# Layer 0 of a four-layer vision network on one core: the norm's broadcast in two steps, and other due times for its streams and its last two samples

## Chip, core and metric

One core of a Trainium2 chip runs the whole program in one launch: all layers, batch 8, everything in fp32. The core has a matrix engine (TensorE, "PE" in the profile), a vector engine (VectorE, "DVE"), a scalar engine (ScalarE, "ACT"), a general engine (GpSimd, "POOL"), a queue engine that mostly issues transfers (SyncE, "SP"), and 16 DMA engines that move data between the memory and the on-chip buffers. The metric is device time in microseconds (us) of one launch; lower is better. Five runs give the time before.

## The reference, cut to what matters

The input is `x[8, 256, 32, 32]`; the output has the same shape. Layer 0, the only one that the change edits, is this (batch norms, `_bn`, are folded into scales and shifts):

```python
def _ln(x, w, b):
    r = lax.rsqrt(jnp.mean(x * x, axis=1, keepdims=True) + LN_EPS)
    return x * r * w[:, None, None] + b[:, None, None]

def _attention(x, ...):                     # 4 heads, key 32, value 64, N = 1024 positions
    qkv = _bn(_conv1x1(x, qkv_w), ...)
    attn = softmax(einsum('bhkn,bhkm->bhnm', q, k) * SCALE)
    out = einsum('bhdm,bhnm->bhdn', v, attn)
    pe = _bn(_dwconv3(v_img, pe_w), ...)    # 3x3, one filter per channel
    return _bn(_conv1x1(out + pe, proj_w), ...)

def _edffn(x, pi_w, dw_w, fft_p, po_w):
    x = _dwconv3(_conv1x1(x, pi_w), dw_w)   # 256 -> 1024 channels, then 3x3 per channel
    x = gelu(x[:, :512]) * x[:, 512:]
    x = _conv1x1(x, po_w)                   # 512 -> 256
    return irfft2(rfft2(patches8x8(x)) * fft_p)

def _forward(x, ...):
    x = x + gamma1 * _attention(_ln(x, norm1_w, norm1_b), ...)
    return x + gamma2 * _edffn(_ln(x, norm2_w, norm2_b), pi_w, dw_w, fft_p, po_w)
```

The norm `_ln` divides by the root mean square over the 256 channels: the sum runs over channels, and the result `r`, one number per position, is needed again in every channel. Layer 1 is a deformable convolution; further layers are attention and mixtures of experts. They matter here only because the first steps of layer 1 are issued while layer 0 ends.

## The kernel before

**Tiling.** A sample is a tile of 128 partitions by 2 x 1024: 256 channels in two halves (`KC = 2`), 1024 positions (`N`), worked on in halves of 512 (`HF`). Layer 0 is the function `fast0` (line 1110 on). It is written as Python generators: each is a *stream* of work for one sample, cut into *units* by `yield`. The streams are:

- `attention()` (`main`): for each sample, each half of the queries and each of 8 key tiles, two units: first the scores `s` (line 1393, four matmuls) and their exponentials `e` on ACT (L1399); then, one key tile late, the sums of the exponentials on DVE (`sum`, L1349 and L1353) and the values `A` (L1357, eight matmuls). That makes 32 units a sample (`T = 32`). After a half, `finish` runs beside the next steps: copy `A` to `av` (ACT), the denominators `D` (PE, L1372, from `sum`), their reciprocal `rr` by Ln and Exp (ACT, L1376 and the next), `av` times `rr` and `o` plus `av` (both DVE), two units later the projection `proj` (PE), the residual `x+av` (DVE, L1387) and the store to a DRAM buffer `mid`.
- `before_attention(b)`: load the sample (SP), norm it, project v, q and k (`qkv`, line 78 is the helper that issues it; the copies out are L1280), transpose v (`vT`, L1297), and do the 3x3 convolution of v on PE (`pe`, L1324) from a shifted copy `thrice` that twelve transfers on SP fill.
- `before_gates(b)`: load `mid`, norm it. `gates(b)`: eight blocks of 128 channels, each a 1x1 convolution (`pi`, PE), its copy out (`hp`, ACT, L1438) and a 3x3 depthwise convolution on DVE (`a`, first tap on ACT at L1239, eight taps on DVE at L1246). Pairs of blocks pass through gelu (ACT) into `st` and are multiplied by the partner block (DVE), then stored. In the last sample blocks 1 and 7 take the convolution on PE instead, as matmuls with diagonals (`dw`).
- `transforms(b)`: for each quarter of the sample, load the gated values `hc` and the residual `xc`, 1x1 convolution `po` (PE, L1491), forward transform `fwd` (PE), its gain (`u`, DVE, L1501), back transform `back` (PE, L1506), add to `xc` (DVE), store.

**The norm** is one helper for both places, `normed` (L1214 to L1235). It squares the sample (ACT, L1217); unit; sums the squares over channels with a matmul whose result lies as 64 equal rows per half (`ms`, PE, L1222) and takes `r` = 1/root by Ln and Exp (ACT, L93 and L94); unit; then for each half a matmul with a row of ones spreads a row of `r` to all partitions (`rb`, PE, L1231) and ACT copies it out (L1234) over the first square tile, which the profile names `v` in the first norm and `sq` in the second; last, one DVE product over the whole sample makes `xn` (L1235). All small results of PE in layer 0, `rb` and `D` and `back` and `pi` among them, take their bank of PSUM (PE's result memory) from one pool, `own["X"]`. It has two banks during attention, so a third result waits until one of the last two has been read out. After attention it has four.

**The order.** Nothing runs these streams in parallel by itself: the function `by_time` plays one unit after another, always of the stream whose *due time* is smallest, and adds the stream's *pace* to its due time. Time is counted in units of `main`, which starts at 0 with pace 1, so sample b's attention lies at 32b to 32b + 32, and the 256 units of all eight end near 258. The engines' instruction orders come from this order, through a scheduler that may still move an instruction ahead of others on its engine; only instructions marked `pinned` (gelu and its table load) keep their place. Each stream is given as (first due time, pace, generator):

```python
(T * (b - 1) - 2, 32 / 21, before_attention(b)) if b > 1 else (11 * b, 1.0, before_attention(b)),
(T * (b + 1) + 7.4, 0.9, before_gates(b)),
(T * (b + 1) + 10.5, 32 / 44, gates(b)),
(T * (b + 2) + 11.5, 2, transforms(b)),
```

So in the middle of the layer four samples are in work at once: while b attends, b+1 is being prepared, b-1 is in its norm and gates, and b-2 in its transforms. Ten units of `before_attention(0)` are played ahead of all (`next(streams[1][2])`). When `main` ends, attention's buffers are given back, and what is left of the last streams is played together with `net.head()`, due at T*B + 1 with pace 2. That is the first part of layer 1: its weight loads on SP and ACT's queue, memsets on POOL, the load of its first sample, that sample's first convolution (`c`) and group norm (`gn`), and so on, until a mark (`HOLD`) from which it needs layer 0's space.

Of the kernel before, what the change touches and what calls it, by code (L numbers as in the profile page):

```python
# [18 lines left out]
B = 8  # L19
# [117 lines left out]
def img(ap):  # L137
    return ap.rearrange("p (h w) -> p h w", w=IMG)
# [954 lines left out]
def by_time(streams, until=None):  # L1093


    due = [list(s) for s in streams]
    while due:
        d = min(due, key=lambda d: d[0])
        try:
            next(d[2])  # L1100
            d[0] += d[1]
        except StopIteration:
            due.remove(d)
            if d[2] is until:
                break
    return due
# [3 lines left out]
def fast0(net, io):  # L1110
# [7 lines left out]
    with ExitStack() as ctx, ExitStack() as att:  # L1118
# [35 lines left out]
        def bank(name):  # L1154
            return own["X"].tile([P, HF], F32, tag="X", name=name)
# [51 lines left out]
        def sc(i):  # L1207
            return s[:, i : i + 1]

        def sh(i):  # L1210
            return t[:, i : i + 1]

        def normed(xn, x, sq):

            squares = [sq(k) for k in range(KC)]
            for k in range(KC):
                nc.scalar.activation(squares[k], x[:, k, :], AF.Square)  # L1217
            yield
            ps = bank("ms")
            for k in range(KC):  # L1220
                for h in range(2):
                    nc.tensor.matmul(  # L1222
                        ps[64 * h : 64 * h + 64], lhsT=net.mean64, rhs=squares[k][:, bass.ts(h, HF)],
                        start=(k == 0), stop=(k == KC - 1),
                    )
            r = one.tile([P, HF], F32, tag="r", name="r")
            net.rsqrt(r, ps, net.eps6)
            yield
            for h in range(2):
                pr = bank("rb")  # L1230
                nc.tensor.matmul(  # L1231
                    pr, lhsT=net.unit[64 * h : 64 * h + 1, :], rhs=r[64 * h : 64 * h + 1, :], start=True, stop=True
                )
                nc.scalar.copy(squares[0][:, bass.ts(h, HF)], pr)  # L1234
            nc.vector.tensor_tensor(xn, x, squares[0].unsqueeze(1).to_broadcast([P, KC, N]), ALU.mult)  # L1235

        def depthwise(out, src, taps):
# [31 lines left out]
        def before_attention(b):  # L1269
            xn = aone.tile([P, KC, N], F32, tag="xn", name="xn")  # L1270
            nc.sync.dma_start(out=xn, in_=io.src[b])
            yield
            v = aone.tile([P, KC, N], F32, tag="v", name="v")
            yield from normed(xn, xn, lambda k: v[:, k, :])
            yield
            def projected(d, w, j, norm):
                for h in range(2):
                    ps = bank("qkv")
                    net.linear(ps, w, xn, bass.ts(j, P), bass.ts(h, HF))
                    nc.scalar.activation(d[:, bass.ts(h, HF)], ps, AF.Identity, scale=sc(norm), bias=sh(norm))  # L1280

            for c in range(KC):
                projected(v[:, c, :], wv, c, 2 + c)
                yield
            for d, (j, name) in ((qs, (0, "q")), (ks, (1, "k"))):
                d[b] = atwo.tile([P, N], F32, tag=name, name=name)
                projected(d[b], wqk, j, j)
                yield

            va = vas[b] = atwo.tile([P, NT, KC, P], F32, tag="va", name="va")  # L1290
            for t4 in range(0, NT, 4):
                for t2 in (t4, t4 + 2):
                    ps = bank("vT")
                    for i in range(2):
                        for c in range(KC):
                            lo = i * C + c * P
                            nc.tensor.transpose(ps[:, lo : lo + P], v[:, c, bass.ts(t2 + i, P)], net.ident)  # L1297
                    nc.scalar.copy(va[:, t2 : t2 + 2].rearrange("p t c d -> p (t c d)"), ps)
                yield

            o = os[b] = atwo.tile([P, KC, N], F32, tag="o", name="o")
            for c in range(KC):
                for h in range(2):

                    thrice = aone.tile([96, 4, HF], F32, tag="thrice", name="thrice")
                    edge = thrice[0:32, :, :IMG] if h == 0 else thrice[64:96, :, HF - IMG :]
                    nc.gpsimd.memset(edge, 0.0)  # L1307
                    for j in range(3):
                        n = HF * h + IMG * (j - 1)
                        lo, hi = max(0, n), min(N, n + HF)  # L1310
                        for g in range(4):
                            nc.sync.dma_start(
                                out=thrice[32 * j : 32 * j + 32, g, lo - n : hi - n],
                                in_=v[32 * g : 32 * g + 32, c, lo:hi],
                            )
                    yield
                    ps = bank("pe")
                    for j, s_ in enumerate((0, -1, 1)):
                        for g in range(4):
                            to, fr = (  # L1320
                                img(a)[:, :, max(0, -d_) : IMG - max(0, d_)]
                                for a, d_ in ((ps[32 * g : 32 * g + 32], s_), (thrice[:, g, :], -s_))
                            )
                            nc.tensor.matmul(  # L1324
                                to, lhsT=wpe[:96, c, s_ + 1, g, :], rhs=fr, start=(j == 0), stop=(j == 2)
                            )
                    nc.scalar.activation(
                        o[:, c, bass.ts(h, HF)], ps, AF.Identity, scale=sc(4 + c), bias=sh(4 + c)
                    )
                    yield  # L1330
                yield
# [87 lines left out]
        def before_gates(b):  # L1419
            xn = xs[b] = one.tile([P, KC, N], F32, tag="xn2", name="xn2")  # L1420
            nc.sync.dma_start(out=xn, in_=mids[b])
            yield

            def square(k):
                return five.tile([P, N], F32, tag="a", name="sq") if k else one.tile([P, N], F32, tag="sq", name="sq")

            yield from normed(xn, xn, square)
            yield
# [89 lines left out]
        T = 32  # L1518
        main = attention()
        streams = [(0, 1, main)]  # L1520
        for b in range(B):
            streams += [
                (T * (b - 1) - 2, 32 / 21, before_attention(b)) if b > 1 else (11 * b, 1.0, before_attention(b)),
                (T * (b + 1) + 7.4, 0.9, before_gates(b)),
                (T * (b + 1) + 10.5, 32 / 44, gates(b)),
                (T * (b + 2) + 11.5, 2, transforms(b)),
            ]
        for _ in range(10):
            next(streams[1][2])
        rest = by_time(streams, until=main)  # L1530
        att.close()
        own["X"], own["diag"] = io.pool(ctx, "f0t", 4, PSUM), io.pool(ctx, "f0d", 2)
        by_time(rest + [[T * B + 1, 2, net.head()]])

# [1422 lines left out]

GENERAL = [layer0, layer1, layer2_attention, layer2_ffn, layer3_attention, layer3_experts]  # L2960
LAYERS = [fast0, fast1, fast2, fast2f, fast3, fast3e]
LEAST, MOST = 1e-25, 1e25

# [265 lines left out]
```

## Time and profile before

| | us |
|---|---|
| five runs | 4276.41, 4264.66, 4272.24, 4272.69, 4262.2 |
| their median | 4272.24 |
| the profiled execution, its own time | 4274.56 |
| its span, first to last instruction | 4272.80 |
| layer 0 up to the last attention projection | 0 to 1279.39 |
| last projection to the last sample's first `pi` | 1279.39 to 1318.70 |
| one middle sample, `rb` to `rb` | 662.26 to 823.14 |

How to read the profile's lines, here and in the prediction: in the totals each engine has its busy time, its share of the span and its number of instructions; PEld is the loading of weights into PE, which lies beside its matmuls. In a timeline each line is start, duration, engine, source line, operation, "output<-inputs", partitions and elements, and how many like instructions the line stands for; a bracket gives the idle time of that engine just before, and what ended it. In a table of windows each line is a stretch of time, its length, then the busy time (and count) of PE, PEld, DVE, ACT and POOL, the mean granted clock of PE (1.00 is full speed), the busy share of the DMA engines, and the GB/s that they moved. The same view by whole stretches, for orientation:

```profile
340.00:501.00 161.00, 150.41 (x736) 57.65 (x732) 129.76 (x119) 88.47 (x112) 0.78 (x4) 0.96 0.26 82
501.00:662.00 161.00, 151.09 (x760) 58.67 (x753) 130.37 (x121) 93.42 (x119) 0.78 (x4) 0.98 0.27 85
662.00:823.00 161.00, 151.04 (x759) 58.55 (x753) 130.34 (x122) 93.36 (x119) 0.79 (x4) 0.98 0.27 85
823.00:984.00 161.00, 151.92 (x760) 58.67 (x755) 131.21 (x123) 94.84 (x120) 0.79 (x4) 0.98 0.27 85
```

The stretches are of one sample's length each. PE is busy for all but 8 to 11 us of 161, DVE for all but some 30.

### The profile page before, as it was taken

Reading aid. Unit: us, or ns where it says so; the run is one execution under the profiler, and the core shown is the slowest. Engines: PE = TensorE matmul, PEld = TensorE weight load, DVE = VectorE, ACT = ScalarE, POOL = GpSimd, SP = SyncE. Lnnn points to the kernel's source line nnn. Section 1 sums busy time; section 2 is a strip of 40 time slices with the busy share of each in tenths; the row PEclk is TensorE's granted clock in tenths of the full one; section 3 lists DMA queues with packets and bytes.
Section 4 is the critical chain, followed back from the end, with each engine's and each line's share of the span. In section 5 each row is a group of like instructions: output and inputs, shape, how many; then the busy total and the mean of one; then the engine's idle time right before and its main releaser. Section 6 shows DMA issues by size and latency. Waiting matters only on the chain. (4 is left out here: it accounts for less than half of the span.)

```text
span 4272.8 us, 53170 instructions
## 1 busy us (share of the span) xinstructions
PE 3968.6 (93%) x20006; PEld 1923.1 (45%) x20006; DVE 2295.6 (54%) x3979; ACT 2262.1 (53%) x3030; POOL 564.0 (13%) x645
## 2 busy tenths in 40 slices
PE   7999999999897899989999987989899999999997
PEld 3223333333333444445444444654344434445986
DVE  2368878878896577762222326853223333314455
ACT  3455555555554466653343345634656666666554
POOL 0000000000000000000000002531000151114763
PEclk9989999999998999999999998999999999999998
DMA  2222232232213101110010012541700041026676
GB/s 87 64 69 71 73 103 79 72 106 72 82 55 123 65 32 61 42 47 6 20 40 20 20 40 72 156 130 30 224 31 1 35 133 42 33 87 199 194 243 222
DMA packets 190637, 350.34 MB, mean 82 GB/s; under 512 B 24121, under 2 KB 134669, under 8 KB 178853
## 3 DMA queue, kind: packets, MB, share of 16 engines
q1 hardware_dynamic: 167124, 294.10, 21.2%
q0 software_dynamic: 19440, 46.45, 3.3%
q10 hardware_dynamic: 3808, 6.29, 0.4%
q8 instruction: 162, 2.65, 0.3%
q14 instruction: 103, 0.84, 0.1%
HBM read 175.15 MB, written 153.89 MB: 77 GB/s over the span
## 5 line engine op out<-in xcount | busy, mean ns | idle before, releaser
L2683 ACT ACTIVATE e<-s,five 128x1024 f32<-128x1024 f32 x512 | 539.3, 1111 | 281.2 <-PE s L2677 280.1
L1246 DVE SCALAR_TENSOR_TENSOR a<-hp,w_f_vec,a 128x961 f32<-128x961 f32 (+1 forms) x496 | 608.9, 1234 | 109.4 <-ACT a L1239 101.0
L2677 PE MATMUL s<-q,k 32*128 32x512 f32 x2048 | 348.9, 642 | 17.5 <-ACT e L2683 12.2
L1353 DVE TENSOR_TENSOR sum<-sum,e 128x1024 f32<-128x1024 f32 x192 | 230.8, 1221 | 154.4 <-ACT e L1399 154.4
L1399 ACT ACTIVATE e<-s 128x1024 f32<-128x1024 f32 x256 | 249.7, 1023 | 92.7 <-PE s L1393 83.1
L2661 PE MATMUL A<-e,v 128*32 128x512 f32 x2048 | 278.5, 608 | 0.0
L1357 PE MATMUL A<-e,va 128*32 128x512 f32 x2048 | 277.5, 624 | 0.0
L78 PE MATMUL pi<-xn,w_l_wpi 128*128 128x512 f32 x512 | 246.0, 622 | 14.8 <-ACT u L1500 9.2
L2677 PEld LDWEIGHTS s<-q,k 32*128 32x128 f32 x2048 | 111.5, 183 | 180.8 <-issue 96.5
L1393 PE MATMUL s<-q,k 32*128 32x512 f32 x1024 | 181.5, 645 | 2.4 <-ACT e L1399 2.4
L1724 PE MATMUL pos<-pos,w_f_sel 64*128 64x512 f32 x576 | 163.0, 631 | 8.5 <-ACT ay L1746 3.9
L78 PEld LDWEIGHTS pi<-xn,w_l_wpi 128*128 128x128 f32 x512 | 95.5, 197 | 154.1 <-issue 115.7
L1026 POOL DMA_INDIRECT res<-y,to x149 | 148.6, 998 | 106.9 <-DVE y L2854 49.4
L2830 PE MATMUL h<-xk,w 128*128 128x128 f32 x1192 | 149.0, 279 | 11.4 <-DVE xk L2816 11.4
L2830 PEld LDWEIGHTS h<-xk,w 128*128 128x128 f32 x1192 | 147.2, 195 | 16.3 <-DVE xk L2816 11.4
L2799 ACT COPY w<-w_l3f_w 128x512 f32 x149 | 92.6, 625 | 114.6 <-PE h L2830 110.6
L1438 ACT ACTIVATE hp<-pi,pib 128x512 f32<-128x512 f32 x128 | 87.2, 690 | 117.4 <-PE pi L78 117.4
L1324 PE MATMUL pe<-thrice,w_f_wpe 96*32 96x496 f32 (+1 forms) x768 | 129.9, 607 | 20.7 <-DMA thrice<-v 14.1
L1307 POOL MEMSET thrice<- 32x128 f32 x32 | 6.3, 196 | 1081.3 <-PE pe L1324 1061.3
L2850 PE MATMUL y<-w_l3f_w,hid 128*128 x596 | 144.3, 385 | 0.3 <-issue 0.3
L1357 PEld LDWEIGHTS A<-e,va 128*32 128x32 f32 x2048 | 61.8, 113 | 178.2 <-issue 177.3
L1026 POOL DMA_INDIRECT so<-xl,rows x128 | 129.6, 1013 | 93.6 <-issue 49.5
(408 smaller groups left out, 7067.7 us busy)
## 6 DMA issues: line engine op xcount, KB each, us to landing
x<-d SPq DMA_DIRECT2D x31, 1024.0 KB
xs<-so SPq DMA_DIRECT2D x73, 260.0 KB
so<-zero SPq DMA_DIRECT2D x5, 3380.0 KB
thrice<-v SPq DMA_DIRECT2D x256, 64.0 KB
gated<-st SPq DMA_DIRECT2D x32, 512.0 KB
hc<-gated SPq DMA_DIRECT2D x32, 512.0 KB
d<-x SPq DMA_DIRECT2D x16, 1024.0 KB
xl<-mox SPq DMA_DIRECT2D x64, 256.0 KB
```

Source lines behind the costliest of these rows:

```text
L78: self.nc.tensor.matmul(ps, lhsT=w[:, i, m], rhs=src[:, i, cols], start=(i == 0), stop=(i == k - 1))
L1026: made = self.nc.gpsimd.indirect_dma_start(**args)
L1246: nc.vector.scalar_tensor_tensor(to, fr, taps(t_), to, ALU.mult, ALU.add)
L1353: nc.vector.tensor_tensor(half, half, e[j], ALU.add)
L1357: nc.tensor.matmul(state["A"][32 * h : 32 * h + 32, c, :], lhsT=vas[b][:, kt, c, 32 * h : 32 * h + 32], rhs=e[h // 2][:, h % 2, :], start= ...
L1393: nc.tensor.matmul(ss[h // 2][:, h % 2], lhsT=ks[b][32 * h : 32 * h + 32, bass.ts(kt, P)], rhs=qs[b][32 * h : 32 * h + 32, bass.ts(gq, HF) ...
L1399: nc.scalar.activation(es[i][j], ss[j], AF.Exp, scale=SCALE)
L1724: nc.tensor.matmul(ps[:, bass.ts(h, HF)], lhsT=sel[r, t, xy, :], rhs=poss[b][r, :], start=True, stop=True)
L2661: nc.tensor.matmul(A[32 * h : 32 * h + 32], lhsT=v[:, kt, c * P + 32 * h : c * P + 32 * h + 32], rhs=e[:, h, :], start=first, stop=last,)
L2677: nc.tensor.matmul(ss[h // 2][:, h % 2], lhsT=k[32 * h : 32 * h + 32, c, bass.ts(kt, P)], rhs=q[32 * h : 32 * h + 32, c, bass.ts(hh, HF)], ...
L2683: nc.scalar.activation(e[:, 2 * j : 2 * j + 2], ss[j], AF.Square, scale=SCALE, bias=five)
L2830: nc.tensor.matmul(ps[:, j, m], lhsT=ws[j][:, k, bass.ts(m, P)], rhs=xk[:, j, k], start=(k == 0), stop=(k == KC - 1),)
```

## The change

It edits only `normed` and the end of `fast0`:

```diff
                 nc.scalar.copy(squares[0][:, bass.ts(h, HF)], pr)
+                if h == 0:
+                    yield
             nc.vector.tensor_tensor(xn, x, squares[0].unsqueeze(1).to_broadcast([P, KC, N]), ALU.mult)
...
             streams += [
-                (T * (b - 1) - 2, 32 / 21, before_attention(b)) if b > 1 else (11 * b, 1.0, before_attention(b)),
-                (T * (b + 1) + 7.4, 0.9, before_gates(b)),
+                (T * (b - 1) - 2, 32 / 22, before_attention(b)) if b > 1 else (11 * b, 1.0, before_attention(b)),
+                (T * (b + 1) + 7.4, 0.7, before_gates(b)),
                 (T * (b + 1) + 10.5, 32 / 44, gates(b)),
                 (T * (b + 2) + 11.5, 2, transforms(b)),
             ]
-        for _ in range(10):
+
+
+        for i, (at, pace) in enumerate(((T * (B - 1) + 10.5, 0.58), (T * B + 5.5, 2))):
+            streams[4 * (B - 2) + 3 + i] = (at, pace, streams[4 * (B - 2) + 3 + i][2])
+        for i, (at, pace) in enumerate(((T * B + 4.2, 0.7), (T * B + 7.3, 32 / 44), (T * B + 40.5, 2))):
+            streams[4 * (B - 1) + 2 + i] = (at, pace, streams[4 * (B - 1) + 2 + i][2])
+        for _ in range(11):
             next(streams[1][2])
         rest = by_time(streams, until=main)
         att.close()
         own["X"], own["diag"] = io.pool(ctx, "f0t", 4, PSUM), io.pool(ctx, "f0d", 2)
-        by_time(rest + [[T * B + 1, 2, net.head()]])
+        by_time(rest + [[T * B + 5, 2, net.head()]])
```

- In `normed` a unit ends behind the first half's broadcast and copy. Other streams' work may now stand between the two `rb` matmuls, and both norms have one unit more.
- `before_attention` gets the pace 32/22 for 32/21, its unit more in the same 32; `before_gates` gets 0.7 for 0.9. Eleven units are played ahead for ten.
- The streams of the last two samples are replaced. `gates(6)` starts when it did and goes at 0.58 for 0.727 a unit; `transforms(6)` starts 6 earlier. `before_gates(7)`, `gates(7)` and `transforms(7)` start 3.2, 3.2 and 3 earlier.
- The head of layer 1 is due at T*B + 5, behind the start of the last sample's norm at T*B + 4.2; before, it was due at T*B + 1, ahead of that norm's T*B + 7.4.

Line numbers of the kernel after are those of before plus 2 from line 1236 on, and plus 8 behind `fast0`.

## The prediction

> **What bounds the kernel now.** I read the page's totals first, then the layer's end by stages, then one sample of the middle engine by engine. The first two lines are the page's engine totals and its chain of waits: TensorE (PE) is busy nine tenths of the span and nothing else is near that.
>
> ```profile
> PE 3968.6 (93%) x20006; PEld 1923.1 (45%) x20006; DVE 2295.6 (54%) x3979; ACT 2262.1 (53%) x3030; POOL 564.0 (13%) x645
> ...
> PE 17%; DMA 2%; DVE 1%; issue 1%; POOL 0%; ACT 0%; DVEq 0%; SPq 0%; POOLq 0%; ACTq 0%
> ```
>
> So time can come only from places where PE waits or is given a slow clock. In layer 0 there are two kinds. The first recurs once per sample. The PE timeline (start, duration, operation, idle before and releaser), then VectorE's (DVE):
>
> ```profile
> 823.14 1.03 PE L1231 MATMUL rb<-r,unit 1*128 1x512 f32 x4
> 826.51 1.93 PE L1372 MATMUL D<-sum,unit 128*32 128x512 f32 x8 [2.33 <-ACT v L1234]
> 828.22 2.60 PE L1357 MATMUL A<-e,va 128*32 128x512 f32 x16
> 830.75 1.16 PE L1506 MATMUL back<-w_l_inv,u 128*128 128x128 f32 x8
> 831.84 1.14 PE L1393 MATMUL s<-q,k 32*128 32x512 f32 x8
> 832.91 3.70 PE L78 MATMUL qkv<-xn,w_f_wv 128*128 128x512 f32 x8
> ...
> 844.13 3.70 PE L78 MATMUL pi<-xn,w_l_wpi 128*128 128x512 f32 x8 [0.97 <-ACT v L1280]
> ```
> ```profile
> 822.93 0.69 DVE L1501 TENSOR_TENSOR u<-u,w_l_gam 128x512 f32<-128x512 f32 x1
> 824.19 5.05 DVE L1246 SCALAR_TENSOR_TENSOR a<-hp,w_f_vec,a 128x961 f32<-128x961 f32 x4 [0.57 <-ACT a L1239]
> 829.15 2.28 DVE L1235 TENSOR_TENSOR xn<-xn,v 128x2048 f32<-128x2048 f32 x1
> ```
>
> Both rb banks are full, so D waits 2.33 us for the copy out of the first. The product xn is ready at 831.4, and qkv never waits for it. After the gap PE is slow, as the granted clock (third column from the right) of two windows at the same place one sample earlier shows:
>
> ```profile
> 663.00:666.00 3.00, 0.67 (x6) 0.16 (x8) 2.62 (x3) 3.00 (x5) 0.00 (x0) 0.97 0.00 0
> 666.00:669.00 3.00, 3.00 (x20) 0.73 (x16) 2.96 (x3) 1.29 (x3) 0.00 (x0) 0.50 0.00 0
> ```
>
> D and A then take 4.24 us (826.51 to 830.75) against 2.72 elsewhere (588.96 to 591.68): 1.5 lost. The gap costs 3.85 us in all. The second kind is the end of the layer, by stages: last sample but one up to the last proj, the last norm, two stretches of the last sample's gates and transforms.
>
> ```profile
> 1183.94:1279.39 95.45, 85.80 (x416) 37.79 (x417) 89.75 (x85) 51.92 (x65) 0.00 (x0) 0.97 0.15 49
> 1279.39:1306.63 27.24, 10.85 (x26) 3.89 (x24) 23.25 (x28) 15.38 (x32) 6.01 (x6) 0.75 0.77 289
> 1306.63:1318.70 12.07, 10.74 (x34) 3.19 (x34) 3.43 (x7) 4.54 (x10) 0.00 (x0) 0.68 0.41 145
> 1318.70:1425.57 106.87, 98.39 (x301) 49.72 (x301) 70.52 (x75) 38.78 (x55) 0.00 (x0) 0.95 0.13 45
> 1425.57:1469.91 44.34, 39.80 (x186) 22.71 (x184) 12.38 (x28) 12.05 (x23) 0.50 (x2) 0.96 0.32 103
> ```
>
> DVE is busy 89.75 of 95.45 us in the first: it bounds that stage. In the second PE does 10.85 us of work in 27.24.
>
> **The change, part by part.** The built programs hold the same instructions; only their order differs, from the second norm on until layer 1's early matmuls (after that, by 1520 us, it is the same again). So the time moves by what PE's waits and slow clock change.
>
> *Two-step broadcast, first norm of samples 3 to 7.* The built orders (4 of 5 alike; sample 3 lacks back and xc):
>
> ```
> PE  before  rb rb D A*8 back s*4 qkv            after  rb D A*8 back rb s*4 A*8 qkv
> DVE before  u a*4 xn av xc o xc                 after  u a*3 sum av a o xc xc xn
> ```
>
> Removed: the 3.85 us. Added: on DVE xn now stands behind sum, av, o (1.13 each, 836.67 to 837.80) and two xc (0.34 each, 832.56 to 832.90): 4.1 later, from 833.2 to 835.4. All their inputs are there by then (rr and back's copy before 828.5), so it is queueing, and DVE cannot start earlier: it idles 0.57 at 824.19 for ScalarE (ACT). PE needs 823.14 + 2x0.53 + 0.88 + 1.83 + 1.09 + 1.07 + 1.85 = 830.9, then waits 4.4 for xn, then runs slow as above, 1.5. Net 4.4 + 1.5 - 3.85 = **+2.05** (bounds: +0.55 if the clock stays up; +2.6 if xn slips by half a product more).
>
> [...]
>
> *Behind it.* The second v projection moves to just behind pi (5 A between). It needs pi's bank, and ACT empties it only after the gelu block (838.50 to 843.30, 4.8), two e (1.8) and one hp (0.7), with 0.9 for v's copy: 8.2 after the first projection. PE has s, pi, 5 A: 5.8. Wait 2.4 for 0.97: **+1.4** (0 to +2.9 with a slow stretch).
>
> *Second norm (before_gates).* On DVE x+av (L1387) moves from behind 2 a to behind 6: 4.6 later. From its end to the squares, through two transfers on SP's queue, the trace has 692.71 to 700.76 = 8.05. So squares, ms and the queue behind ACT's squares (e, r, then rb's copy) come some 5 late, while PE, with k moved behind ms, arrives earlier; pi then waits for xn once more (about 2). Removed: 0.88 + 0.38 + 1.18 of waits with about 1.5 of slow clock. I take **+1.5** (0 to +5; nearest the low end, since PE's own lateness uses up part).
>
> *Pace 32/22.* po now stands in front of pe and covers the wait for thrice, 14.1 us over 9 places in the waits up to 1160 us; 0.5 to 1.8 in the middle samples: **-1.3**.
>
> Sum per sample 3.65 (from -1.3 to +9), five samples: **+18** (-6 to +45). Samples 0 to 2 have no gates beside the norm; their orders barely change: 0.
>
> *The plan of the last two samples.* With pace 0.58, nine more a and one more st pair stand on DVE before the last o: 98.4 us of DVE work from xn (1181.59) for 87.5 (the built orders, counted at the trace's steps: a 1.14, sum, av, o and x+av 1.13, st 0.61, u 0.60, xc 0.34, xn 2.21). With the 4.6 that DVE waits for its first a, o ends at 1284.6 for 1277.3. x+av follows 8 later as before, 1292.6. Then sample 6's own chain (1164.98 to 1183.94, 19) replaces the old 33.3 (1285.38 to 1318.70), because xn's load no longer follows five weight loads on SP. But it follows layer 1's x load and one d store that waits for xc (1.5), and three c matmuls stand between ms and rb whose weight load, now behind a gated store, took 8.9 from issue to c before: I add 4 in all (1.5 to 8). First pi of the last sample: 1315.6 for 1318.7, **-3** (-6 to +1). By then 9 off, one acc and two gn (9x0.27 + 1.06 + 0.3 = **+3.8**) are still to do. Up to pos before takes 151.2 (1318.70 to 1469.91) for 137.9 of matmul steps (start to start: pi 0.89, po 0.45, the diagonals' dw 0.87, fwd, z and acc 1.06, back and off 0.27, c 0.49, z_ 0.17); the new order needs no 12.95 us stop of DVE for back behind dw, and I give it 9 of loss for 13.3: **-4.3** (-9 to 0). Four z, eight z_ and four c (7.5) move behind pos, where PE idles 5.9 of 40: **-3**. Sum of the end **-6** (-18 to +6). POOL's order is unchanged; its memsets move with the head and nobody waits for them.
>
> Total +18 - 6 = +12. The profiled execution took 4274.56 (span 4272.80); with 12 it would be 4286.6. It lies 2.3 above the median of the five, so against that: **4284**.
>
> **Rivals.** *Even:* the moved waits cost what the old ones did; x+av and xn are late, but ACT and DVE catch up in DVE's 9 us of idle per sample. For it: the sums of +0.55 and 0 are within the bounds. Against: PE has no slack at the point itself. Then only the end counts: 4272 - 6 = 4266. *Faster:* the two old gaps go and xn's wait stays under 2, so each sample gains 2, and the hole of 27.24 us closes by another 6: 4272 - 10 - 12 = 4250. For it: that hole holds 16 us of idle. Against: DVE's order above. *Slower at the end too:* the last attention half is starved by DVE (D waits for sums behind nine more a, back for u), and the proj's 7 us never come back: -6 becomes +8, 4272 + 18 + 8 = 4298; it decides from the point where PE waits over 4 us for D.
>
> **Chances.** Forecast 0.45 (4280 to 4292), slower at the end 0.13, even 0.19, faster 0.23. A measurement of this kernel tells 0.2% (8.5 us) from no change. Slower 0.58, same 0.19, faster 0.23. The range reaches into both outer cases: 4250 to 4302.
>
> **What would show it.** Right: PE's wait at qkv for xn near 4 us in samples 4 to 7, none at D, a period (rb to rb, 662.26 to 823.14 before) of 163 to 165 us instead of 160.9, the last proj near 1285 plus the lag gathered, the 27.24 us hole shorter. Wrong: xn's wait under 2, a period at or below 160.9, or pi of the last sample over 10 us nearer to the last proj than I reckon.

## The result and the profile after

The changed kernel took 4289.18 us (median of 26 runs) where the kernel before, run beside it, took 4270.84 (median of 47): a ratio of 1.0040 with a 95% interval of 1.0033 to 1.0047, or +17 us (14 to 20). The forecast was +12 and slower. The direction and the size were right; the parts of the sum were not. The split broadcast cost less than half of what it was charged, and the new plan of the end, which was to give back 6, cost about 9 by the stages of the profile. The profiled execution of the changed kernel took 4285.93 us, its span 4284.1. So the two profiled executions differ by 11 us, where the medians differ by 18: that of before lies 3.7 us above its median, that of the changed kernel 3.3 below.

The page's engine totals and its chain of waits, after:

```profile
PE 3948.2 (92%) x20006; PEld 1930.0 (45%) x20006; DVE 2297.3 (54%) x3979; ACT 2263.5 (53%) x3030; POOL 563.2 (13%) x645
...
PE 3%; DMA 1%; DVE 1%; issue 0%; POOL 0%; DVEq 0%; ACT 0%; SPq 0%; POOLq 0%
```

The counts are those of before and the busy times hardly differ; PE is even busy 20 us less in a span 11 us longer. So the added time is waiting. The shares of the chain sum to 21% of the span before and to 5% after, and its pieces lie in the last fifth and the last twentieth; so it says nothing of layer 0.

The PE timeline of a middle sample at the first norm, then VectorE's (columns as before; the product xn, L1235 in the kernel before, is L1237 here):

```profile
819.47 1.90 PE L1359 MATMUL A<-e,va 128*32 128x512 f32 x16
821.30 1.16 PE L1508 MATMUL back<-w_l_inv,u 128*128 128x128 f32 x8
...
824.30 1.92 PE L1359 MATMUL A<-e,va 128*32 128x512 f32 x16
829.94 5.40 PE L78 MATMUL qkv<-xn,w_f_wv 128*128 128x512 f32 x8 [3.72 <-DVE xn L1237]
...
843.59 3.70 PE L78 MATMUL qkv<-xn,w_f_wv 128*128 128x512 f32 x8 [1.72 <-ACT hp L1440]
```
```profile
822.36 1.22 DVE L1351 TENSOR_TENSOR sum<-e 128x1024 f32<-128x1024 f32 x1
823.50 1.22 DVE L1381 TENSOR_TENSOR av<-av,rr 128x1024 f32<-128x1024 f32 x1
824.63 1.25 DVE L1248 SCALAR_TENSOR_TENSOR a<-hp,w_f_vec,a 128x992 f32<-128x992 f32 x1
825.79 1.22 DVE L1382 TENSOR_TENSOR o<-o,av 128x1024 f32<-128x1024 f32 x1
826.93 0.76 DVE L1515 TENSOR_TENSOR xc<-u,xc 128x256 f32<-128x256 f32 x2
827.60 2.29 DVE L1237 TENSOR_TENSOR xn<-xn,v 128x2048 f32<-128x2048 f32 x1
```

D no longer waits. In its place PE waits 3.72 us for xn, and the first projection then takes 5.40 us (granted clock 0.69 from 829.90 to 835.40) where the second takes 3.70 (1.00 from 843.50 to 847.30). The last copy of rb ends at 824.12 (ACT starts it at 823.54, 0.58 long), but DVE does av, a, o and xc before it turns to xn at 827.60: 3.5 us of queue.

All waits of PE over one sample, from the last proj of one to that of the next (line, releaser, total, times, longest), first before, then after:

```profile
PE D L1372 <- ACT v L1234: 2.3, 1, 2.3
PE pe L1324 <- DMA thrice<-v: 1.8, 1, 1.8
PE pi L78 <- ACT u L1500: 1.5, 1, 1.5
PE vT L1297 <- ACT sq L1234: 1.2, 1, 1.2
PE pi L78 <- ACT v L1280: 1.0, 1, 1.0
PE ms L1222 <- ACT k L1280: 0.9, 1, 0.9
```
```profile
PE qkv L78 <- DVE xn L1237: 3.7, 1, 3.7
PE ms L1222 <- ACT sq L1217: 2.3, 1, 2.3
PE qkv L78 <- ACT hp L1440: 1.7, 1, 1.7
PE pi L78 <- ACT u L1502: 1.5, 1, 1.5
PE pi L78 <- DVE xn L1237: 1.2, 1, 1.2
```

Of the old waits shown all but one went, and new ones came. With those too small to show, the waits of a sample went from 10.0 us to 10.9 here, and to 11.5 to 12.1 in the samples beside it.

The end by stages: last attention (last proj of sample 6 to last proj of sample 7), to the last sample's first pi, to layer 1's first pos, and to layer 1's last pos, where layer 1 ends. First before, then after:

```profile
1154.36:1279.39 125.03, 108.71 (x526) 44.29 (x527) 116.71 (x110) 65.09 (x81) 0.00 (x0) 0.94 0.20 69
1279.39:1318.70 39.31, 21.59 (x59) 7.08 (x57) 26.68 (x34) 19.92 (x41) 6.01 (x6) 0.73 0.66 245
1318.70:1469.91 151.21, 138.19 (x486) 72.43 (x485) 82.89 (x103) 50.83 (x78) 0.50 (x2) 0.95 0.19 62
1469.91:1884.11 414.20, 373.99 (x2465) 179.15 (x2464) 324.36 (x497) 269.30 (x369) 0.00 (x0) 0.98 0.11 43
```
```profile
1158.10:1291.23 133.13, 112.72 (x524) 44.69 (x525) 125.37 (x119) 71.08 (x89) 0.00 (x0) 0.92 0.20 70
1291.23:1325.05 33.82, 13.95 (x37) 5.15 (x37) 15.52 (x16) 12.13 (x28) 6.01 (x6) 0.69 0.72 251
1325.05:1479.19 154.14, 134.10 (x476) 70.78 (x476) 82.60 (x109) 49.38 (x78) 0.50 (x2) 0.92 0.19 65
1479.19:1896.98 417.79, 377.15 (x2500) 180.06 (x2499) 326.30 (x500) 271.89 (x374) 0.00 (x0) 0.99 0.11 42
```

From the last proj on, the three stages sum to 604.7 before and 605.8 after: what the earlier start of the last sample gives in the first (5.5 us) is lost in the next two. What stays is the last attention, 8.1 us longer, with DVE busy 125.4 of 133.1 us and nine instructions more in it. The chief waits of PE from the last proj on, after (the one for o ends as the last proj starts):

```profile
PE ms L1222 <- ACT sq L1217: 17.3, 1, 17.3
PE z L1672 <- DVE z L1676: 10.6, 1, 10.6
PE proj L78 <- DVE o L1382: 5.7, 1, 5.7
PE back L1508 <- DVE u L1503: 4.8, 4, 2.8
```

Ahead of the last proj PE stands idle for 5.7 us until the late o is done; that time lies in the last attention, whose 8.1 us more are 4.1 of idle time and 4.0 of busy time of PE (granted clock 0.92 for 0.94). Behind it ms stands 17.3 us behind the squares with nothing to do in between (before, PE waited 10.4 us there for the weights of layer 1's c), and layer 1's z, now in the middle of the last sample's gates, waits 10.6 for a VectorE that is busy with them (10.67 of 10.70 us, 1404.90 to 1415.60).

### The profile page after: what moved, and what is told of

Same layout as the page of the kernel before. It is cut to its first block, busy times and chain, and to the rows that moved or that the text cites. A ratio compares the mean times of both kernels' runs of the same rounds, so it can differ in the third digit from the quotient of the medians.

```text
span 4284.1 us, 53173 instructions
## 1 busy us (share of the span) xinstructions
PE 3948.2 (92%) x20006; PEld 1930.0 (45%) x20006; DVE 2297.3 (54%) x3979; ACT 2263.5 (53%) x3030; POOL 563.2 (13%) x645
## 5 line engine op out<-in xcount | busy, mean ns | idle before, releaser
L1359 PE MATMUL A<-e,va 128*32 128x512 f32 x2048 | 287.3, 611 | 0.0
L78 PE MATMUL pi<-xn,w_l_wpi 128*128 128x512 f32 x512 | 241.3, 614 | 19.9 <-DVE xn L1237 10.6
L1732 PE MATMUL pos<-pos,w_f_sel 64*128 64x512 f32 x576 | 164.8, 633 | 10.4 <-ACT ay L1754 4.7
L78 PEld LDWEIGHTS pi<-xn,w_l_wpi 128*128 128x128 f32 x512 | 94.4, 194 | 157.8 <-issue 110.1
L2598 DVE COPY v<-v 128x1024 f32<-128x1024 f32 x16 | 19.6, 1224 | 212.8 <-PE v L78 212.8
```

Of the source, the lines that this page charges most:

```text
L78: self.nc.tensor.matmul(ps, lhsT=w[:, i, m], rhs=src[:, i, cols], start=(i == 0), stop=(i == k - 1))
L1359: nc.tensor.matmul(state["A"][32 * h : 32 * h + 32, c, :], lhsT=vas[b][:, kt, c, 32 * h : 32 * h + 32], rhs=e[h // 2][:, h % 2, :], start= ...
```

## The experiments

Each ran in five rounds beside the kernel before on the same chip. Chips differ: on some the kernel before took 4317 to 4329 us, and the profiles put the 50 us more behind layer 1 (from layer 2's first av, an attention matmul, to the end 2328 to 2334 us on the one, 2376 to 2387 on the others). So totals are compared only as ratios, and stages of layers 0 and 1 across runs. In the table a middle sample is a quarter of the time from sample 1's last proj to sample 5's; the end is the time from sample 6's last proj to layer 1's last pos.

| kernel | ratio to before (95%) | sample 0's last proj, us | middle sample, us | end, us |
|---|---|---|---|---|
| before | | 205.9 | 160.5 | 729.8 |
| after | 1.0040 (1.0033 to 1.0047) | 202.1 | 162.3 | 738.9 |
| e1 split only | 1.0017 (1.0007 to 1.0026) | 200.7 | 161.5 | 727.1 |
| e2 plan only | 1.0015 (1.0001 to 1.0028) | 206.6 | 158.7 | 738.6 |
| e3 sixth gates only | 1.0041 (1.0029 to 1.0054) | 206.7 | 158.7 | 747.5 |
| e4 head behind norm | 0.9992 (0.9980 to 1.0004) | 205.4 | 159.6 | 722.9 |
| e5 split, first norm | 1.0005 (0.9993 to 1.0018) | 201.4 | 160.4 | 735.1 |
| e6 split, second norm | 1.0017 (1.0003 to 1.0030) | 205.9 | 159.4 | 729.1 |
| e7 plan, head early | 1.0025 (1.0013 to 1.0038) | 204.6 | 158.9 | 751.9 |
| e8 split, product too | 0.9945 (0.9924 to 0.9965) | 195.2 | 159.6 | 728.5 |
| e9 e8, head behind | 0.9967 (0.9956 to 0.9978) | 194.3 | 160.4 | 729.7 |
| e10 product halves only | 0.9946 (0.9928 to 0.9963) | 204.1 | 156.9 | 727.2 |
| e11 changed, product halves | 0.9986 (0.9975 to 0.9996) | 192.7 | 159.6 | 735.6 |
| e12 e10, head behind | 0.9947 (0.9928 to 0.9966) | 202.4 | 156.3 | 727.8 |

**The change in two halves.** e1 takes the first three edits alone:

```diff
                 nc.scalar.copy(squares[0][:, bass.ts(h, HF)], pr)
+                if h == 0:
+                    yield
...
-  32 / 21, before_attention(b)     0.9, before_gates(b)     range(10)
+  32 / 22, before_attention(b)     0.7, before_gates(b)     range(11)
```

> The unit between the two broadcasts in both norms, with the paces 32/22 and 0.7 and eleven units ahead; the last two samples and the head of layer 1 as before. My theory (both halves of the change cost): sample 0 to 5 run as in the changed kernel, so the last proj of sample 6 lies near 1158 (1154.4 before), wait at qkv for xn 3.7 per sample and none at D; the last attention keeps its 125 us, last proj near 1283, first pos near 1474; total +4 to +8 us. Rival 'the split is the whole loss': total +14 to +20, with a last proj above 1290. Rival 'the split costs nothing, the plan is the loss': last proj of sample 6 at or below 1155, total within 3 us of before.

Measured: +7 us (3 to 11). Last proj of sample 6 at 1153.1, last proj 1276.3, first pos 1466.2: all 5 to 8 us sooner than expected, the first of them where the rival 'costs nothing' had it. But this profiled execution lies 6.4 us below the median of its kernel (4270.40 for 4276.84), so the ratio decides. The waits are those of the changed kernel (3.7 at qkv in each middle sample, none at D). A part of the loss, as the theory had it, and not the whole.

e2 takes the rest alone; with the norm undivided its stream keeps 0.9 a unit:

```diff
+        for i, (at, pace) in enumerate(((T * (B - 1) + 10.5, 0.58), (T * B + 5.5, 2))):
+            streams[4 * (B - 2) + 3 + i] = (at, pace, streams[4 * (B - 2) + 3 + i][2])
+        for i, (at, pace) in enumerate(((T * B + 4.2, 0.9), (T * B + 7.3, 32 / 44), (T * B + 40.5, 2))):
+            streams[4 * (B - 1) + 2 + i] = (at, pace, streams[4 * (B - 1) + 2 + i][2])
...
-        by_time(rest + [[T * B + 1, 2, net.head()]])
+        by_time(rest + [[T * B + 5, 2, net.head()]])
```

> The new due times of the last two samples and of the head, with the norm undivided (its stream at 0.9 a unit) and everything else as before. My theory: samples 0 to 5 as before (last proj of sample 6 at 1154.4), the last attention 8 us longer (133 for 125) because DVE has nine more taps in front of the last o, last proj near 1287.5; from there to the first pos 188 for 190.5; total +4 to +8. Rival 'plan is the whole loss': +14 to +20. Rival 'plan pays': first pos at or before 1466, total -4 or less.

Measured: +6 us (0.4 to 12). The stages, last attention, last proj to first pos, first pos to layer 1's last pos:

```profile
1147.68:1280.77 133.09, 112.71 (x524) 44.61 (x525) 125.35 (x119) 71.08 (x89) 0.00 (x0) 0.92 0.19 69
1280.77:1466.02 185.25, 146.69 (x512) 74.69 (x512) 98.10 (x124) 61.51 (x106) 6.50 (x8) 0.89 0.29 100
1466.02:1886.27 420.25, 380.79 (x2499) 182.64 (x2498) 326.37 (x500) 271.76 (x374) 0.00 (x0) 0.98 0.11 42
```

The last attention is 8.1 us longer than before, the next stage 5.3 shorter, layer 1 then 6.1 longer: 8.8 in all. A first pos that comes sooner is no gain if what follows waits; the first pos was a poor mark for the end, and the last one is used from here on. The two halves sum to +13.7, and the change is +17 (14 to 20): no interplay is needed.

**The plan taken apart.** e3 has only the first of the two loops above (sample 6's gates and transforms).

> Of the plan only the first part: gates(6) at 0.58 a unit and transforms(6) six earlier; the last sample's norm, gates and transforms and the head as before. My theory: the last attention is 7 to 9 us longer (DVE), as with the whole plan; behind the last proj less is left of sample 6, but its norm still comes behind the head's loads, so the 27 us stretch with little matmul stays; total +3 to +9. Rival 'the earlier gates are given back in full behind the last proj': total within 2 us. Rival 'DVE is not what holds the last attention': last proj within 2 us of 1279.4.

A miss in size: +17 us (12 to 23). The last attention is 133.0 as expected, but the time from the last proj to layer 1's last pos is also 9.8 longer (614.5 for 604.7). So the earlier gates of sample 6 give nothing behind the last proj and cost 8 ahead of it; why the part behind it grew was not taken apart. e4 changes only the head:

```diff
-        by_time(rest + [[T * B + 1, 2, net.head()]])
+        by_time(rest + [[T * B + 8.2, 2, net.head()]])
```

> Of the plan only the order of the last norm and the head: the head of layer 1 is due at T*B + 8.2, behind the start of the last norm at T*B + 7.4, which keeps its time, as do gates and transforms. My theory: the load of xn no longer stands behind five weight loads, so the first pi of the last sample comes 5 to 12 us sooner after the last proj (39.3 before), and the layer ends 3 to 8 us sooner; the total follows, -2 to -8. Rival 'the transfer was not what the norm waited for': the 39.3 us stay within 2, total within 2 us. Rival 'what the head loses it loses in layer 1': first pi sooner, but first pos not, total 0 or above.

The first pi came 32.3 us after the last proj instead of 39.3, and the end is 6.9 shorter; the ratio gives -3 us with an interval from -8.5 to +1.7, so the total says no more than that it is likely. e7 is the reverse: e2 with the head left at T*B + 1.

> The plan of the last two samples without the later head: head at T*B + 1 as before, all else as in the run of the plan alone. My theory (the order of the last norm and the head is what the plan gains): the last proj at 1281 to 1287 as with the whole plan, but from there to the first pos 192 to 198 us instead of 185, and the total +11 to +16. Rival 'the head's place is nothing, the earlier norm alone gains': 184 to 187 us behind the last proj, total as with the whole plan, +5 to +8.

+11 us (6 to 16) and 194.8 us behind the last proj: the theory's numbers, though its last attention was 139.3 us and the interval reaches the rival's +8. In the plan, sample 6's part costs, the head's place wins some of it back.

**The split, norm by norm.** e5 gives the unit to the first norm alone (with 32/22 and eleven units), e6 to the second alone (with 0.7):

```diff
-        def normed(xn, x, sq):
+        def normed(xn, x, sq, split=False):
...
+                if h == 0 and split:
+                    yield
```

> The unit between the broadcasts in the first norm alone (before_attention at 32/22, eleven units ahead), the second norm and the end as before. My theory: the waits at qkv for xn (3.7) and at the second qkv for its bank (1.7 to 2.0) stand, with the slow matmuls behind the first; D's 2.3 is gone; the wait at ms for the squares is under 1.5; the first four samples end 3 to 5 us sooner as in the run with both splits; a middle sample takes 161 to 162.5 us, and the total is +3 to +7. Rival 'the second norm is what costs': middle samples at 158 to 160, total -5 to 0.

> The unit between the broadcasts in the second norm alone (before_gates at 0.7 a unit), the first norm and the end as before. My theory: D's wait of 2.3 stands and none at qkv for xn; ms waits 2 to 3 for the squares; a middle sample takes 159.5 to 161 us; the total is 0 to +4. Rival 'the second norm is what costs': middle samples at 161.5 or more, total +6 to +9. Rival 'the second split pays': middle samples at 158 or less, total -5 or less.

e5: +2 us (-3 to +8); the waits at qkv are 3.7 and 1.7 and D's is gone, as expected, but ms waits 3.9 for the squares where under 1.5 was expected, and a middle sample takes 160.4. e6: +7 us (1 to 13), but its profile shows a middle sample of 159.4 and the shortest run to layer 1's end of the two. The profiled execution of e5 lies 6.4 us above its median and that of e6 5.3 below, so ratio and profile disagree by more than the effect, and which norm costs more stays open.

**The product.** e8 is e1 with the product cut in two, each half behind its own copy:

```diff
                 nc.scalar.copy(squares[0][:, bass.ts(h, HF)], pr)
+                half = squares[0][:, bass.ts(h, HF)].unsqueeze(1).to_broadcast([P, KC, HF])
+                nc.vector.tensor_tensor(xn[:, :, bass.ts(h, HF)], x[:, :, bass.ts(h, HF)], half, ALU.mult)
                 if h == 0:
                     yield
-            nc.vector.tensor_tensor(xn, x, squares[0].unsqueeze(1).to_broadcast([P, KC, N]), ALU.mult)
```

> As the run with both splits and the end of before, but the product xn is split too: each half of the positions is multiplied right behind its own broadcast's copy. My theory (xn queues on DVE behind work of others, and that wait is the loss): the wait at qkv for xn falls from 3.7 to under 1.2, a middle sample takes 157.5 to 159.5 us, and the total falls from +6 to -4 to +1. Rival 'the extra loss is the slow clock and the second bank, not the product': the middle samples stay at 161 or more and the total at +4 to +9. Rival 'two short products disturb DVE's depthwise taps and push o late': a proj wait shows, total above +9.

-24 us (-33 to -15), far better than expected. e11 puts the same edit into the changed kernel.

> The changed kernel with the product alone by halves, each right behind its own broadcast's copy. My theory (the whole product queued on DVE is what turned the two-step broadcast into a loss): qkv's wait for xn falls from 3.7 to under 1.2 in the middle samples and from 8.3 at sample 2, the last attention stays at 133 us (that is the sixth sample's gates), and the ratio falls from 1.004 to 0.9965 to 0.999. Rival 'the gain of the halves belongs to the old end': ratio above 1.001.

1.0040 became 0.9986 (0.9975 to 0.9996), as the theory had it. The PE timeline of e11 at the first norm of the same sample:

```profile
805.55 1.92 PE L1360 MATMUL A<-e,va 128*32 128x512 f32 x16
807.40 1.98 PE L78 MATMUL qkv<-xn,w_f_wv 128*128 128x512 f32 x4
810.13 1.98 PE L78 MATMUL qkv<-xn,w_f_wv 128*128 128x512 f32 x4 [0.74 <-DVE xn L1236]
```

The first projection starts without a wait, the second half of it waits 0.74 instead of 3.72, and each half, four matmuls, takes 1.98 us (eight took 3.70 in after, at a granted clock of 1.00). The second projection waits 2.08 us for its bank and then takes 5.40 us in three of the four middle samples. The last attention is still 132.5 us and the end 735.6. But e10, the same cut in the kernel *before*, with no unit between the broadcasts and no due time changed, was run too:

```diff
                 nc.scalar.copy(squares[0][:, bass.ts(h, HF)], pr)
+                half = squares[0][:, bass.ts(h, HF)].unsqueeze(1).to_broadcast([P, KC, HF])
+                nc.vector.tensor_tensor(xn[:, :, bass.ts(h, HF)], x[:, :, bass.ts(h, HF)], half, ALU.mult)
-            nc.vector.tensor_tensor(xn, x, squares[0].unsqueeze(1).to_broadcast([P, KC, N]), ALU.mult)
```

> The kernel before with the product alone by halves, each right behind its own broadcast's copy: no unit between the broadcasts, no due time changed. My theory (in the middle samples of before nobody waits for xn, so halves gain only at the start, where qkv waits 3.48, 1.47 and 2.62 for it): the first last proj 2 to 4 us sooner, middle samples unchanged with D's 2.3 still there, total -3 to -9, ratio 0.998 to 0.9993. Rival 'the halves are the whole gain': ratio at or below 0.9955. Rival 'two products cost DVE more than one': ratio above 1.0005.

A clear miss: 0.9946, the gain of e8 without the split. In its middle samples nobody waits for xn, and D's 2.3 is still there:

```profile
PE D L1373 <- ACT v L1234: 2.3, 1, 2.3
PE pi L78 <- ACT u L1501: 1.5, 1, 1.5
PE vT L1298 <- ACT sq L1234: 1.2, 1, 1.2
...
PE pe L1325 <- DMA thrice<-v: 0.5, 1, 0.5
```

So the halves are worth 0.54% on the kernel before, 0.72% on e1 and 0.54% on the changed kernel, and only on the last two can a wait for xn in the middle samples be the reason. And e11's ratio alone does not show that this wait was the loss, since e10 gains as much without it. Where e10 gains can be told: the time from sample 0's last proj to sample 1's is 153.3 us for 159.3, and a middle sample 156.9 for 158.7 to 160.5, a gain of 2.4 on their mean. Most of that is seen in the scores `s` behind the second norm. Their eight matmuls of one unit, first before, then in e10:

```profile
714.75 1.12 PE L1393 MATMUL s<-q,k 32*128 32x512 f32 x2
719.87 1.12 PE L1393 MATMUL s<-q,k 32*128 32x512 f32 x2
721.50 1.13 PE L1393 MATMUL s<-q,k 32*128 32x512 f32 x4
```
```profile
702.80 1.14 PE L1394 MATMUL s<-q,k 32*128 32x512 f32 x8
```

Two or four of them take as long as all eight together. Before, the order has one unit in three pieces with other matmuls between them, in each of the 20 middle samples of before, e2, e3, e4 and e7; in e10 and e12 no unit is in pieces. A sample's 128 score matmuls then take, from start to start and without waits, 17.2 us for 19.3. That is PE's busy time, and no list of waits shows it. Why halving the product moved them is not shown. Between samples 0 and 1 the wait for xn falls from 2.62 to 1.38 us and the projection behind it from 5.27 to 3.67: 2.8 of the 6.0, and the rest was not taken apart.

In the total e8 equals e10 (0.9945 and 0.9946, each known to some 0.002). By stages they differ: e8 is 8.1 us ahead at sample 1's last proj (349.2 for 357.3) and 2.8 behind at sample 5's (987.7 for 984.9), and e9, e11 and e12 show the same. So with the product halved the two-step broadcast gains at the start and still costs some 3 us in each middle sample. There PE waits no longer than in e10 (7.7 us a sample for 8.3), but the score matmuls, in more pieces, take 22.0 us for 17.2.

**Adding the two gains.** e9 is e8 with e4's head, e12 is e10 with it.

> Both splits with the product by halves, and the head of layer 1 due at T*B + 8.2, behind the start of the last norm; the last two samples' streams as before. My theory (the gains are in different places and add): layer 0 up to the first pos 28 to 34 us shorter than before, the ratio 0.990 to 0.9945. Rival 'the head's later place only shifts its work into layer 1': the ratio within 0.001 of that without it (0.9945).

> The kernel before with the product by halves, and the head of layer 1 due at T*B + 8.2, behind the start of the last norm. Everything else as before. Theory 'the two gains add': the stretch from the last proj to layer 1's last pos is 4 to 9 us shorter than with the halves alone (605 there), and the ratio is 0.9915 to 0.9935. Rival 'c then stands before the norm's matmuls and waits for its weights, 13 to 16 us, so the head's place gives nothing once the layer ends sooner': that stretch within 3 us or longer, ratio 0.994 to 0.997.

They don't add. e9 is 0.9967, e12 0.9947, and the end is 729.7 and 727.8 us for 728.5 and 727.2 without the later head. Behind e12's last proj PE waits chiefly here:

```profile
PE c L1615 <- DMA w_l_w<-in_l_w_dram: 15.5, 1, 15.5
PE dw L1262 <- ACT hp L1439: 5.7, 2, 4.9
PE back L1507 <- DVE u L1502: 4.3, 4, 3.2
```

Layer 1's c stands in front of the norm's matmuls and waits 15.5 us for the weights that were put back, as the rival had it. The numbers fit the rival, but that this wait takes the gain is not shown: c waits 10.4 us in before and e10 too, and 13.6 in e4, where the end did get shorter. Three versions share the best ratio and beat both kernels: e8, e10 and e12; e10 needs the least.

## Why the forecast held, and which parts did not

1. *Two-step broadcast, the step itself: right.* D's gap gone, xn queued behind sum, av, o and xc: 3.72 us of wait forecast as 4.4, the slow clock behind it 1.70 (5.40 for 3.70, granted 0.69 for 1.00) forecast as 1.5. In e11, with the product halved, the wait is 0.74 and the first projection takes 1.98 us for each half. Against the old gap with its slow D and A (2.33 + 1.70, with 4.41 for 2.71 us, granted 0.61 for 1.00) the step is +1.4; forecast +2.05.

2. *Per sample: mis-sized, and so the +18.* The second v wait is +0.8 to +1.0 (forecast 1.4), the second norm's waits +1.5 (2.3 to 3.2 at ms and 1.2 at pi, for 0.9, 0.4 and 1.2 before; forecast 1.5), the slow clock not counted (ms itself took 2.02 to 3.55 us in five samples of after, 1.94 in before; granted 0.54 at the 3.55), the covered thrice -1.8 in this sample and -0.9 on the mean of the 20 middle samples named under e10 (forecast -1.3): some +2.0 to +2.9 with the first. Measured by stages it is +2.6: 161.9, the mean of after and e1, less 159.3, the mean of the five kernels whose middle is that of before (before, e2, e3, e4, e7). The profiled execution of before lies at the top of these five, with sample 6's last proj at 1154.4 where the five average 1149.6, so that the two profiles alone understate the loss. The prediction's premise that time moves only by PE's waits and its slow clock was too narrow: PE's busy time moved with the order too (a sample's score matmuls 20.7 us for 19.3, those of pe 10.9 for 13.8, both from start to start without waits, against longer qkv and A). These mostly cancel here, so the waits give about the right sum. The forecast took 3.65, and five samples; there are four, since the next interval (146.9 for 147.1) shows nothing.

3. *"Samples 0 to 2 ... 0" was wrong.* With the first norm's unit and eleven units ahead, sample 0's last proj comes at 200.7 to 202.1 instead of 204.6 to 206.7, and sample 1's at 360.5 to 362.0 instead of 363.8 to 365.9: -3.8 on the mean, so that the whole split is +6 at sample 6's last proj (1155.6 for 1149.6) and +7 by e1's ratio. Not +18.

4. *The end was wrong in sign: -6 forecast, +9.1 measured.* First, o: xn to o takes 105.9 us (1185.23 to 1291.09) for 95.8 (1181.59 to 1277.35), +10.1 where +7.3 was reckoned. The prediction's own count of DVE's work was 10.9 longer (98.4 for 87.5), but 1181.59 + 87.5 + 4.6 is 1273.7 and not 1277.35, so 3.7 of what DVE takes in before was left out of the new sum. From x+av's end to the first pi it takes 26.4 us (1298.68 to 1325.05) for 33.3, where 23 was reckoned. So the first pi is +2.6 late (8.1 less 5.5), not 3 early. Second, from there to pos it is 154.1, not 147.7: the 4.3 that DVE's spared stop and the 3 that the moved z and c were to give are gone; PE waits 10.6 us at z for DVE, which no wait of before answers to, and 2.7 at po for a load. Third, layer 1 behind the first pos is 3.6 longer, which the sum did not have at all. 2.6 + 2.9 + 3.6 = 9.1.

5. *The rivals.* "Faster" and "even" fell on the xn wait, which they needed under 2 or caught up. "Slower at the end too" has the right sign for the end (it gave +8), but not by its mechanism: D waits 2.5 us in three places, 1.2 at most, not over 4. The loss is o's lateness on DVE, which the forecast itself had named and thought recovered.

The total of 12 for 17 was therefore luck, two errors that mostly cancel: 11 too much for the split, 15 too little for the end.

## What to carry to other kernels

A wait that goes away on one engine is only gone if the next consumer's input comes sooner too: here the broadcast was freed, but the product that uses it sat 3.5 us deep in another engine's queue, and halving that product gained more than the whole change lost. But it gained as much in the kernel before, whose middle samples never wait for the product, and most of what a middle sample gained there was seen in the score matmuls, no longer cut into pieces (17.2 us a sample for 19.3): here the new order changed an engine's busy time too, so compare start-to-start times of like groups, and not only waits. Work moved ahead of a point can cost there and give nothing back behind it: with sample 6's gates earlier (e3) the last attention took 133.0 us for 125.0, and the time behind the last proj was 9.8 longer too. Measure an end by the last event of what follows, not by the first.

## What the runs showed of the hardware

The slow clock after one and the same gap is not one number. In the eight profiles with the undivided first norm, samples 3 to 6, D and A behind the 2.33 us gap took 4.0 to 4.4 us in 25 of 32 cases, 5.28 in six, and 2.71, no loss at all, in one. At sample 2, behind a gap of the same length, it was 2.71 in two of the eight, e6 and e7, and 4.15 to 5.28 in the others. The one of the 32, in e4, with the granted clock (third column from the right) of the window beside it:

```profile
820.89 1.06 PE L1372 MATMUL D<-sum,unit 128*32 128x512 f32 x8 [2.33 <-ACT v L1234]
821.77 1.90 PE L1357 MATMUL A<-e,va 128*32 128x512 f32 x16
```
```profile
821.00:824.00 3.00, 3.00 (x27) 0.96 (x27) 2.93 (x4) 1.56 (x3) 0.00 (x0) 1.00 0.01 3
```

The clock stayed at 1.00 there, against 0.50 in the prediction's window. Periods of unchanged middle samples ran from 157.8 to 161.0 us with such differences among their causes, which is why a single profile could not tell 2 us per sample. Of the 40 gaps of 2.33 us 37 were followed by a slow stretch (in before the granted clock over D and A was 0.50 at sample 2 and 0.61 to 0.63 at samples 3 to 6); what decides between the three outcomes of one and the same gap is not shown.
